# A graph attention kernel: who issues the single rows of the last two batches, and how the last batch's products and copies are laid out

## The chip, the cores and the metric

The kernel runs on one core of a Trainium2 chip. The metric is the device time of one execution in microseconds (us). Each run is one execution. A profile of one execution stands beside it; its times are counted from the start of its span.

## The reference

The reference is one layer of graph attention with a residual. There are 12,500 nodes of 128 values and 412,500 edges, sorted by their target `dst`, each with 64 values of its own. There are four heads of 32 values.

```python
h = jnp.maximum(_layernorm(x, axis=-1), 0.0)
h = (h @ W_node.T).reshape(num_nodes, H, HD)
e = (edge_attr_64 @ W_edge.T).reshape(num_edges, H, HD)
att = jnp.sum(concat([h[src], h[dst], e], -1) * a, axis=-1)
att = jnp.where(att > 0, att, 0.2 * att)
m = jnp.maximum(segment_max(att, dst), 0.0)
ex = jnp.exp(att - m[dst])
denom = segment_sum(ex, dst) + (num_edges - deg)[:, None] * jnp.exp(-m)
out = x + segment_sum((ex / denom[dst])[:, :, None] * h[src], dst)
```

## The kernel before

**The data.** A first phase writes a table of one row of 144 values (576 bytes) per node: for each of the four heads 32 values of `h`, two ones and a source logit (35 values, `AW`), and then four target logits. The main phase goes over the edges. 128 edges make a tile, 7 tiles a chunk (461 chunks), and 7 chunks a batch: 66 batches, 0 to 65. The last batch, 65, has six chunks, and the sixth of these has only three tiles. A batch's source rows lie in a tile `hs` with an edge per partition; three buffers of `hs` are used in turn.

**How a batch's rows come in.** Most come by GpSimd (POOL): one indirect DMA gathers the 128 rows of a tile (L636, in `gather`). In batches from 3 on, the first two tiles of an even batch (256 rows) and the first one of an odd batch (128 rows) are left to `row_by_row` (L658 to L662): the addresses are loaded into registers, up to 32 at a time (L658), and each row is then a DMA of its own (L662), issued by the sync engine (SP) or by ScalarE (ACT). A DMA is issued by the engine in whose program it stands, in the order of that program. The constants: `SPROWS` 112, `FRONT` 64, `ACTROWS` 80. In iteration b of the main loop, SP issues up to 64 rows of batch b+1 ahead of `load_near` (L585), then, behind the loads of `eft` (L576, L577), the rest of batch b+1 and rows of batch b+2, up to 112 in all, and leaves 80 rows of batch b+2 over. ACT issues these 80 at the end of iteration b, behind everything else that ACT does in that iteration. So the 256 rows of batch 64 are issued as 112 by SP and 80 by ACT in iteration 62, and 64 by SP in iteration 63; the 128 of batch 65 as 48 by SP and 80 by ACT in iteration 63. In iteration 64 SP has no rows to issue.

**What is done with a batch b.** Each engine takes its instructions in order.

- `weigh` (L718): VectorE (DVE) waits until the rows have landed (`landed`, L670), adds source and target logits (L746), and goes through a leaky unit (L751, L754), two scans along the edges of a target (L757, L759) and a subtraction (L760). ACT takes the exponential (L762). Beside it DVE makes L766. DVE then transposes the result back (L768, L770, L772). `load_pen` (L677, by SP) fetches the next batch's marks of where a target begins, once L766 has read the old ones.
- `scatter` (L813): DVE multiplies the rows by the weights, chunk by chunk (L822), and TensorE (PE) sums the products by target with a matrix `hot` of 0 and 1 (L829).
- For the next batch ACT spreads the target logits over `pick` (L594, once `load_near` has landed), DVE chooses among them (`choose`, L598 to L611) and makes `hot` (`mark`, L714), and PE makes the edges' share `z` (L695).
- `collect` (ACT, L851) copies each chunk's sums from PSUM into `r`, one copy of 32 partitions for each head and chunk. `merge` (L863 to L900) runs along the chunks and adds to the accumulator `acc`. In iterations 62 to 64 both stand at the end of the batch's own iteration. `finish` (L971 to L993) turns finished targets into output rows; a store (L996, by SP) and the next load of `x` (L956, by SP) follow.

**The last batch** has a path of its own, `end_in_parts` (L774): its first four tiles of each chunk (`EARLY`) are done as part 0 and the other three as part 1, so that part 0 can begin while part 1's rows are on their way. For each part DVE weighs (the lines of `weigh_part`) and multiplies (L796). PE makes for each chunk and tile one product of `hot` (128 by 32) with the whole row of 140 values (L802), into 32 partitions at position `at` of PSUM, four chunks in one tile `pa`. ACT then copies 32 partitions by 35 values for each chunk and head into `r` (L810): 24 copies for part 0, and 20 for part 1, where the sixth chunk has no tiles and DVE clears its place in `r` (L807). These copies stand, in the program, ahead of the next part's `weigh_part`. `merge` (from L863) and `finish` come behind it. In `finish` of this end PE makes 16 products at positions `s * W` that change from one product to the next (L988).

Of the kernel before, what the change touches and what calls it, by code (L numbers as in the profile page):

```python
# [9 lines left out]
F32 = mybir.dt.float32  # L10
# [6 lines left out]
ENG = mybir.EngineType  # L17

P = 128
# [4 lines left out]
H = 4  # L24
# [7 lines left out]
CB = 2 * SB - 1  # L32
NBT = -(-NCH // CB)
# [6 lines left out]
W = 32  # L40
G = 4
# [12 lines left out]
AW = HD + 3  # L54
HB = HD + 1
EROW = H * AW
ROW = EROW + H
SPLIT = 2 * AW
RUN = (G - 1) * ROW + SPLIT
# [11 lines left out]
ACTROWS = 80  # L71
# [4 lines left out]
def tiles_of(c):  # L76

    return 0 if c >= NCH else T if c < NCH - 1 else LAST
# [12 lines left out]
def by_row(b):  # L91

    return (2 if b % EVERY == 0 and b < NBT - 1 else 1) if LOOSE < b < NBT else 0


def merges():
# [36 lines left out]
def kernel(  # L133
# [12 lines left out]
    nc = tc.nc  # L146
# [87 lines left out]
    with (  # L234
# [210 lines left out]
        pa = pp1.tile([P, 2 * H], F32, name="pw")  # L445
# [105 lines left out]
    ps = stack.enter_context(tc.tile_pool(name="ps", bufs=1, space=bass.MemoryType.PSUM))  # L551
# [99 lines left out]
    def row_by_row(s, engine, kind, n):  # L651

        last = s.left
        s.left = max(0, last - n)
        some = last - s.left
        while last > s.left:
            first = max(s.left, last - RL, (last - 1) // P * P)
            _, at = nc.values_load_multi_w_load_instructions(  # L658
                row_at[s.b - 2:s.b - 1, first:last], engines=[kind], min_val=0, max_val=(NB * P - 1) * WIDE,
                skip_runtime_bounds_check_because="a src is below N, and N at most NB * P")  # L660
            for i, v in enumerate(at, first):
                by_itself(engine.dma_start(s.hs[i % P:i % P + 1, i // P, :].bitcast(U8),  # L662
                                           table_b[ds(v, WIDE)].rearrange("(o c) -> o c", o=1)),
                          f"lone{s.b}", lone_sems, lone_done, s.b % ROWSEMS)
            last = first
        return n - some
# [107 lines left out]
    def end_in_parts(s):  # L774

        nc.vector.memset(s.pen[:, EARLY * P:EARLY * P + 1], -BIG)
        spans = ((0, EARLY), (EARLY, T))
        r = work.tile([P, AW * (MC + 1)], F32, name="r")
        r = r[:, :AW * (len(spans) * s.chunks + 1)].rearrange("p (d c) -> p d c", d=AW)
        breaks = work.tile([P, s.chunks, len(spans)], F32, name="breaks")  # L780
        nc.vector.memset(breaks, 0.0)
        nc.vector.tensor_copy(breaks[:, :, 0], new[:, s.c0:s.c0 + s.chunks])
        by_chunk = s.hs[:, :, :EROW].rearrange("p (t q) k -> p q t k", q=CB)
        for i, (t0, t1) in enumerate(spans):
            if i:
                landed(nc.vector, "late", late_sems, late_done, 0, s.hs[:, EARLY * CB:, :], s.ends[:, :, :, :])
                weigh_part(s, t0, t1, None)
            else:
                weigh(s, None)
            got = []  # L790
            for q in range(s.chunks):
                held = min(tiles_of(s.c0 + q), t1)
                if held <= t0:
                    continue
                rows = by_chunk[:, q, t0:held, :].rearrange("p t (h k) -> p t h k", h=H)[:, :, :, :HB]
                nc.vector.tensor_tensor(  # L796
                    rows, rows, ex_ps[:, t0:held, q * H:(q + 1) * H, None].to_broadcast([P, held - t0, H, HB]), op=OP.mult)
                if q % G == 0:
                    pa = ps.tile([P, RUN], F32, name="pa", bufs=3)
                at = q % G * W  # L800
                for t in range(t0, held):
                    nc.tensor.matmul(pa[at:at + W, :EROW], s.hot[:, t, q, :], s.hs[:, t * CB + q, :EROW],  # L802
                                     start=(t == t0), stop=(t == held - 1), tile_position=(0, at))
                got.append((q, pa[at:at + W, :]))
            for q in range(s.chunks):
                if tiles_of(s.c0 + q) <= t0:
                    nc.vector.memset(r[:, :, 1 + q * len(spans) + i], 0.0)  # L807
            for q, pa in got:
                for h in range(H):
                    nc.scalar.copy(r[h * W:(h + 1) * W, :, 1 + q * len(spans) + i], pa[:, h * AW:(h + 1) * AW])  # L810
        return r, breaks

    def scatter(s):  # L813
# [240 lines left out]
    def batch(b):  # L1054
        if b not in batches:
            s = batches[b] = Batch()
            s.b = b
            s.c0 = chunk_of(b)
            s.chunks = chunk_of(b + 1) - s.c0
        return batches[b]  # L1060
# [13 lines left out]
    with tc.manual_schedule():  # L1074
        for k in range(AHEAD):
            batch(k).ends = early[k]
        load_near(batch(0))
        batch(0).hs = raw[0]
        load_pen(batch(0))
        load(batch(0))  # L1080
        open_rows(batch(1))
        clear_rows(batch(1))
        gather(batch(1))
        begin(batch(0))
        load(batch(1))
        spread(batch(0))
        choose(batch(0))
        begin(batch(1))
        measure_late(batch(1))
        for b in range(NBT - 1):  # L1090
            s = batch(b)
            batches.pop(b - 2, None)
            before = batches[b - 1] if 1 <= b <= NBT - ALONE else None
            soon = b >= NBT - ALONE
            if AHEAD <= b + 3 < NBT:
                batch(b + 3).ends = index(b + 3)
            front = 0
            if b:
                front = FRONT - row_by_row(batch(b + 1), nc.sync, ENG.SP, FRONT)
            load_near(batch(b + 1))  # L1100
            if before and merge_of(b - 1)[1] == b - 1:
                for b0, n, behind in parts():
                    if behind == b - 1 and not held_x:
                        held_x[b0] = load_part(work, b0, n)
            if b:
                gather(batch(b + 1), scattered.get(b - 2))
            if b + 2 < NBT:
                load(batch(b + 2))
            if b + 2 < NBT:
                open_rows(batch(b + 2))  # L1110
            if b:
                more = max(SPROWS - front, batch(b + 1).left)
                more = row_by_row(batch(b + 1), nc.sync, ENG.SP, more)
                if b + 2 < NBT:
                    row_by_row(batch(b + 2), nc.sync, ENG.SP, min(more, max(0, batch(b + 2).left - ACTROWS)))
            weigh(s, before)
            load_pen(batch(b + 1))
            if b < NBT - 2:
                mark(s)
            for store in stores:  # L1120
                store()
            stores.clear()
            if b == 4 + NG:
                add_windows(counts)
            scatter(s)
            if b == 0:
                rows_late(batch(1))
            spread(batch(b + 1))
            if before:
                close(before, b)  # L1130
            dch = load_chunks(b - 2) if 0 <= b - 2 < NG else None
            choose(batch(b + 1))
            if dch is not None:
                highest(b - 2, dch)
            if b >= NBT - 3:
                mark(batch(b + 1))
            if b + 2 < NBT:
                begin(batch(b + 2))
            if b == 2 + NG:
                counts = count_windows()  # L1140
            if b == 1:
                nc.scalar.copy(acc.rearrange("p q d -> p (q d)"), carry_m.to_broadcast([P, NQ * AW]))
            if soon:
                for b0, n, behind in parts():
                    if behind == b and not held_x:
                        held_x[b0] = load_part(work, b0, n)
                for g in range(2):
                    collect(s, g)
                close(s, b)
            if b + 2 < NBT:  # L1150
                clear_rows(batch(b + 2))
                row_by_row(batch(b + 2), nc.scalar, ENG.Activation, ACTROWS)
        s = batch(NBT - 1)
        for store in stores:
            store()
        stores.clear()
        for b0, n, behind in parts():
            if behind == s.b:
                held_x[b0] = load_part(work, b0, n)
        merged[s.b] = end_in_parts(s)  # L1160
        close(s, NBT - 1)
        for store in stores:
            store()
# [5 lines left out]
    ps = stack.enter_context(tc.tile_pool(name="rest_ps", bufs=1, space=bass.MemoryType.PSUM))  # L1169
# [253 lines left out]
```

## Time and profile before

| | us |
|---|---|
| median of 3 runs | 4031.48 (4031.11 to 4036.24) |
| the profiled execution's own time | 4038.12 |
| its span in the profile | 4036.3 |
| busy in it: POOL / DVE / PE / ACT | 3011.5 / 2379.0 / 1471.9 / 875.2 |

The profile's page gives busy time by engine, 40 slices of the span, the chain of work that ended last, and the costliest groups of instructions. The trace behind it can be asked for a timeline: rows with start, duration, engine, line and operation, output and input tiles, the number of instructions merged into the row, and in brackets the idle time before the row and what ended it. PE is TensorE's matmul, PEld its weight load; an engine's name with a q is its queue of register, wait and DMA-issuing instructions (SPq, ACTq). A row of TensorE counts two records for each product that the program writes.

### The profile page before, as it was taken

How to read it: one execution, taken by the hardware profiler on the slowest of the kernel's cores; microseconds unless marked ns; L12 is line 12 of the kernel's file. 1: busy time of each engine (PE TensorE's matmuls, PEld its weight loads, DVE VectorE, ACT ScalarE, POOL GpSimd, SP SyncE). 2: the span in 40 equal slices, each digit the busy share in tenths (PEclk: the TensorE clock that was granted, in tenths of full speed). 3: DMA queues.
4: the chain of work that ended last, by engine and by line, in shares of the span. 5: the costliest groups of instructions: out<-in, count | busy, mean ns of one | idle time of the engine just before them, and what ended most of it. 6: DMA issues, size and time to landing. Idle time of an engine off the chain costs nothing.

```text
span 4036.3 us, 45376 instructions
## 1 busy us (share of the span) xinstructions
PE 1471.9 (36%) x3512; PEld 577.0 (14%) x3512; DVE 2379.0 (59%) x4319; ACT 875.2 (22%) x2714; POOL 3011.5 (75%) x3205
## 2 busy tenths in 40 slices
PE   5653334443243243333233234234323324324322
PEld 4311111111011011111011111111101101101101
DVE  8676666656555556546546646555655555655565
ACT  5232221222122212212212212212212211211222
POOL 7777777777777777777777777777777777777771
PEclk8776667776676676677576667666667667667666
DMA  8444444434434443334443343443443444343430
GB/s 223 121 102 114 117 109 110 101 93 103 109 90 109 108 110 91 101 88 107 108 110 93 100 103 91 108 109 95 99 107 90 105 108 109 87 105 89 109 92 23
DMA packets 287741, 418.29 MB, mean 104 GB/s; under 512 B 83154, under 2 KB 204430, under 8 KB 287410
## 3 DMA queue, kind: packets, MB, share of 16 engines
q0 software_dynamic: 100128, 230.32, 25.1%
q1 hardware_dynamic: 163696, 174.62, 14.8%
q10 hardware_dynamic: 23586, 10.39, 1.1%
q14 instruction: 301, 2.47, 0.2%
q8 instruction: 30, 0.49, 0.1%
HBM read 399.53 MB, written 15.51 MB: 103 GB/s over the span
## 4 chain that ended last, share of the span: by engine, by line
POOL 50%; issue 19%; DVE 6%; SPq 6%; ACTq 5%; PE 4%; ACT 2%; DMA 1%; DVEq 0%; POOLq 0%
POOL hs L636 50%; ACTq L662 4%; SPq L662 4%; PE pa L829 3%; DVE hs L822 2%; PE z L695 1%; SPq L658 1%; ACTq L658 1%; DMA hs<-table,ends 1%; ACT r L851 1%; ACT both L762 1%; DVE pick L611 1%; DVE hot L714 1%; DVE acc L900 1%; ACT up L986 1%
## 5 line engine op out<-in xcount | busy, mean ns | idle before, releaser
L636 POOL DMA_INDIRECT hs<-table,ends x3062 | 2938.8, 960 | 928.3 <-issue 924.7
L829 PE MATMUL pa<-hs,hot 128*128 128x502 f32 x1820 | 926.2, 673 | 2411.8 <-DVE hs L822 2333.8
L829 PEld LDWEIGHTS pa<-hs,hot 128*128 128x128 f32 x1820 | 396.3, 222 | 2933.8 <-issue 2863.7
L851 ACT COPY r<-pa 32x35 f32<-32x35 f32 x1820 | 380.0, 209 | 1968.7 <-issue 1882.8
L746 DVE TENSOR_TENSOR logits<-hs,pick 128x196 f32<-128x196 f32 (+1 forms) x67 | 32.9, 491 | 1017.2 <-DVEq L670 1016.6
L822 DVE TENSOR_TENSOR hs<-hs,exr 128x924 f32<-128x924 f32 x455 | 472.3, 1107 | 0.0
L695 PE MATMUL z<-eft,wa 128*32 128x512 f32 (+3 forms) x1056 | 443.6, 556 | 28.3 <-DMA eft<-in_ef 28.3
L611 DVE COPY_PREDICATED pick<-exr,lw 128x3136 f32<-128x3136 int32 x66 | 239.8, 3633 | 47.4 <-ACT pick L594 47.3
L611 DVE COPY_PREDICATED pick<-exr,pick 128x1568 f32<-128x1568 int32 (+3 forms) x198 | 230.6, 1165 | 6.8
L762 ACT ACTIVATE both<-a 32x224 f32<-32x224 f32 (+2 forms) x268 | 103.2, 385 | 599.2 <-DVE a L760 529.1
L594 ACT COPY pick<-lw 128x3136 f32<-128x3136 f32 x66 | 184.8, 2800 | 81.8 <-ACTq L670 80.3
L768 DVE STREAM_TRANSPOSE exr<-both 128x224 f32<-128x224 f32 (+1 forms) x67 | 28.3, 423 | 236.0 <-ACT both L762 236.0
L695 PEld LDWEIGHTS z<-eft,wa 128*32 128x32 f32 (+1 forms) x1056 | 95.6, 110 | 378.6 <-issue 353.7
L900 DVE TENSOR_TENSOR acc<-acc,a 128x70 f32 x461 | 108.0, 234 | 69.2 <-issue 50.9
L757 DVE TENSOR_TENSOR_SCAN up<-pen_sb,z 32x896 f32<-32x896 f32 (+1 forms) x67 | 133.3, 1990 | 11.9 <-DMA pen_sb<-pens 9.6
L714 DVE TENSOR_TENSOR hot<-exr,key 128x448 f32<-128x448 f32 (+1 forms) x260 | 129.0, 558 | 9.3 <-PE pa L829 2.3
L759 DVE TENSOR_TENSOR_SCAN m<-pen_sb,up 32x896 f32<-32x896 f32 (+1 forms) x67 | 132.6, 1979 | 2.3
L751 DVE TENSOR_TENSOR a<-z,zst 32x224 f32<-32x224 f32 (+2 forms) x268 | 101.0, 377 | 9.9 <-DVE zst L748 0.5
L766 DVE SCALAR_TENSOR_TENSOR both<-pen_sb,m 32x224 f32<-32x224 f32 (+2 forms) x268 | 100.8, 376 | 2.7
L986 ACT COPY up<-a 32x224 f32<-32x224 f32 (+1 forms) x224 | 74.5, 332 | 35.4 <-DVE a L978 28.7
L246 POOL DMA_INDIRECT hs<-in_x,ends x67 | 63.5, 948 | 20.5 <-issue 20.1
L754 DVE SCALAR_TENSOR_TENSOR z<-a 32x896 f32<-32x896 f32 (+1 forms) x67 | 72.1, 1075 | 2.3
(187 smaller groups left out, 1057.0 us busy)
## 6 DMA issues: line engine op xcount, KB each, us to landing
hs<-table SPq DMA_DIRECT2D x6992, 0.6 KB
eft<-in_ef SPq DMA_DIRECT2D x66, 1344.0 KB
hs<-table ACTq DMA_DIRECT2D x5040, 0.6 KB
hs<-table,ends POOLq DMA_INDIRECT x3062, 2.6
lw<-near SPq DMA_DIRECT2D x461, 64.0 KB
eft<-in_ef SPq DMA_DIRECT2D x66, 224.0 KB
pen_sb<-pens SPq DMA_DIRECT2D x66, 98.1 KB
table<-rows ACTq DMA_DIRECT2D x9, 648.0 KB
```

Of the source, the lines that this page charges most:

```text
L594: nc.scalar.copy(pick[:, :, :s.chunks, :], lw[:, None, :s.chunks, :n].to_broadcast([P, T, s.chunks, n]))
L611: nc.vector.copy_predicated(pick[:, :, :s.chunks, :n], bit[:, :, :, None].to_broadcast([P, T, s.chunks, n]), more)
L636: load = nc.gpsimd.indirect_dma_start(out=s.hs[:n, t * CB + q, :], out_offset=None, in_=table[:, :], in_offset=bass.IndirectOffsetOnAxis(a ...
L662: by_itself(engine.dma_start(s.hs[i % P:i % P + 1, i // P, :].bitcast(U8), table_b[ds(v, WIDE)].rearrange("(o c) -> o c", o=1)), f"lone{s. ...
L695: s.made = own_half(s, nc.tensor.matmul(s.z[:, part], wa3[:n, j, :], s.eft[:n, j, part], start=(j == 0), stop=(j == SB - 1)))
L714: nc.vector.tensor_tensor(s.hot[:, :, q0:q0 + n, :].rearrange("p t q r -> p q t r"), rows_ps[:, None, None, :].to_broadcast([P, n, T, W]), ...
L757: on_half(s, nc.vector.tensor_tensor_scan(up[:, e0:e1], s.pen[:, e0:e1], z, 0.0, op0=OP.add, op1=OP.max))
L762: nc.scalar.activation(both[g * R:(g + 1) * R, 0, t0:t1, :], grouped(att, g), AF.Exp)
L822: nc.vector.tensor_tensor(rows, rows, ex_ps[:, :, q * H:(q + 1) * H, None].to_broadcast([P, T, H, HB]), op=OP.mult)
L829: scattered[s.b] = nc.tensor.matmul(pa, s.hot[:, t, q0:q0 + G, :].rearrange("p q r -> p (q r)"), flat[:, at:at + RUN], start=(t == 0), sto ...
L851: nc.scalar.copy(to, pa[row:row + W, k:k + AW])
L900: nc.vector.tensor_tensor(cols, cols, put[:, i0 + i, :, :], op=OP.add)
```

## The change

There are two edits.

- **Rows.** A new function `act_rows` gives ACT 80 rows in batches up to 63 as before, 40 in batch 64 and none in batch 65. SP takes what is left over, by the rules that stand. Batch 64's rows are then issued as 112 by SP and 40 by ACT in iteration 62, and 64 and 40 by SP in iteration 63; batch 65's as 8 by SP in iteration 63, behind those 40, and in iteration 64 as 64 ahead of `load_near` and 56 behind it, all by SP.
- **The last batch.** For each chunk and tile, four products, one for each head, take the place of one: `hot` with 35 values each, at the head's 32 partitions. All chunks of a part then lie side by side in one tile `pa`, and one ACT copy of 128 partitions by 210 values (`keep`) takes the place of a part's 24 or 20. Part 0's copy stands behind part 1's `weigh_part` in the program. For the chunk without tiles in part 1, DVE clears its place in `pa` instead of in `r`.

```diff
+def act_rows(b):
+    return ACTROWS if b < NBT - 2 else ACTROWS // 2 if b < NBT - 1 else 0
...
     def end_in_parts(s):
...
+        sums = []
+        def keep(i):
+            nc.scalar.copy(r[:, :, 1 + i::len(spans)], sums[i])
         for i, (t0, t1) in enumerate(spans):
             if i:
                 landed(nc.vector, "late", late_sems, late_done, 0, s.hs[:, EARLY * CB:, :], s.ends[:, :, :, :])
                 weigh_part(s, t0, t1, None)
             else:
                 weigh(s, None)
-            got = []
+            if i:
+                keep(i - 1)
+            pa = ps.tile([P, RUN], F32, name="pa", bufs=3)
+            sums.append(pa[:, :s.chunks * AW].rearrange("p (q d) -> p d q", d=AW))
             for q in range(s.chunks):
                 held = min(tiles_of(s.c0 + q), t1)
                 if held <= t0:
+                    nc.vector.memset(sums[i][:, :, q], 0.0)
                     continue
...
-                if q % G == 0:
-                    pa = ps.tile([P, RUN], F32, name="pa", bufs=3)
-                at = q % G * W
                 for t in range(t0, held):
-                    nc.tensor.matmul(pa[at:at + W, :EROW], s.hot[:, t, q, :], s.hs[:, t * CB + q, :EROW],
-                                     start=(t == t0), stop=(t == held - 1), tile_position=(0, at))
-                got.append((q, pa[at:at + W, :]))
-            for q in range(s.chunks):
-                if tiles_of(s.c0 + q) <= t0:
-                    nc.vector.memset(r[:, :, 1 + q * len(spans) + i], 0.0)
-            for q, pa in got:
-                for h in range(H):
-                    nc.scalar.copy(r[h * W:(h + 1) * W, :, 1 + q * len(spans) + i], pa[:, h * AW:(h + 1) * AW])
+                    for h in range(H):
+                        nc.tensor.matmul(pa[h * W:(h + 1) * W, q * AW:(q + 1) * AW], s.hot[:, t, q, :],
+                                         s.hs[:, t * CB + q, h * AW:(h + 1) * AW],
+                                         start=(t == t0), stop=(t == held - 1), tile_position=(0, h * W))
+        keep(len(spans) - 1)
         return r, breaks
...
-                    row_by_row(batch(b + 2), nc.sync, ENG.SP, min(more, max(0, batch(b + 2).left - ACTROWS)))
+                    row_by_row(batch(b + 2), nc.sync, ENG.SP, min(more, max(0, batch(b + 2).left - act_rows(b + 2))))
...
-                row_by_row(batch(b + 2), nc.scalar, ENG.Activation, ACTROWS)
+                row_by_row(batch(b + 2), nc.scalar, ENG.Activation, act_rows(b + 2))
```

## The prediction

> **What bounds the kernel now.** I read the costliest groups first, then POOL's timeline near the end.
>
> ```profile
> L636 POOL DMA_INDIRECT hs<-table,ends x3062 | 2938.8, 960 | 928.3 <-issue 924.7
> 3852.88 0.95 POOL L636 DMA_INDIRECT hs<-table,ends  x1 [0.30 <-issue]
> 3912.87 0.95 POOL L636 DMA_INDIRECT hs<-table,ends  x1 [0.30 <-issue]
> 3914.12 0.95 POOL L636 DMA_INDIRECT hs<-table,ends  x1 [0.19 <-DVE acc L900]
> 3941.13 0.95 POOL L636 DMA_INDIRECT hs<-table,ends  x1 [0.30 <-issue]
> 3959.91 0.94 POOL L636 DMA_INDIRECT hs<-table,ends  x1 [0.30 <-issue]
> ```
>
> POOL issues gathers without a pause: 3062 at 0.96 us, with 0.30 between them. The rows are the last gather of batch 63, the last of 64, and the first, 22nd and 37th of batch 65. The first 22 of these are part 0's, and the last 15 part 1's. POOL ends at 3960.85, and the span at 4036.3. So the last 75 us aren't POOL's, and what the change touches lies there and just before. Next come ACT and DVE in that stretch.
>
> ```profile
> 3847.93 32.92 ACTq L662 DMA_DIRECT2D hs<-table  x80
> 3880.89 1.59 ACT L762 ACTIVATE both<-a 32x224 f32<-32x224 f32 x4 [33.77 <-issue]
> 3917.02 4.25 ACT L986 COPY up<-a 32x96 f32<-32x96 f32 x16 [1.49 <-DVE a L978]
> 3923.41 31.24 ACTq L662 DMA_DIRECT2D hs<-table  x80
> 3954.70 1.59 ACT L762 ACTIVATE both<-a 32x224 f32<-32x224 f32 x4 [33.43 <-issue]
> ...
> 3857.76 0.50 DVE L746 TENSOR_TENSOR logits<-hs,pick 128x196 f32<-128x196 f32 x1 [5.34 <-DVEq L670]
> 3865.64 1.08 DVE L760 TENSOR_TENSOR a<-z,m 32x896 f32<-32x896 f32 x1
> 3882.51 0.43 DVE L768 STREAM_TRANSPOSE exr<-both 128x224 f32<-128x224 f32 x1 [14.29 <-ACT both L762]
> 3922.64 0.37 DVE L746 TENSOR_TENSOR logits<-hs,pick 128x196 f32<-128x196 f32 x1
> 3930.28 1.08 DVE L760 TENSOR_TENSOR a<-z,m 32x896 f32<-32x896 f32 x1
> 3931.29 1.56 DVE L766 SCALAR_TENSOR_TENSOR both<-pen_sb,m 32x224 f32<-32x224 f32 x4
> 3956.32 0.43 DVE L768 STREAM_TRANSPOSE exr<-both 128x224 f32<-128x224 f32 x1 [23.47 <-ACT both L762]
> 3986.79 0.33 DVE L746 TENSOR_TENSOR logits<-hs,pick 128x96 f32<-128x96 f32 x1 [0.21 <-DVEq L670]
> ```
>
> The exponentials (L762) of batches 63 and 64 stand in ACT's queue behind 80 row DMAs each. In batch 64 the argument is ready at 3931.36 (L760's end), but the exponential starts at 3954.70, as the last row has been issued. DVE idles 23.47 us before L768. In batch 63 it idles 14.29 us. Nothing else fills the time, and POOL finishes before DVE needs its rows of batch 65.
>
> **Rows, batch 63's exponential.** 40 row DMAs fewer, at 32.92/80 = 0.41 us with their register loads, take 16.5 us off ACT. Its queue is free at 3864.4, before L760's end at 3866.72. So L762 starts at about 3866.8, 14.1 us earlier, and all that hangs on it in DVE, ACT and PE moves up. How far it carries is set at batch 64's L746, now at 3922.64: without POOL it could start at 3908.5. It needs POOL's last gather of batch 64, which ends at 3913.82. Batch 63 shows how long that takes to be seen: its last gather ended at 3853.83, and L746, which did wait (5.34 us, ended by the wait of L670), started at 3857.76, 3.93 later. So L746 goes to 3917.75: **4.9 us gained**, and the other 9.2 turn into a wait for POOL. The 40 rows that SP takes over are issued from about 3858 (below) and land long before.
>
> **Rows, batch 64's exponential.** ACT's 80 rows in iteration 63 go wholly. L762 starts when L760 has ended, and DVE goes on when L766 has ended (3931.29 + 1.56 = 3932.85). With a pass between engines L768 is at 3933.0 instead of 3956.32: **23.3 us gained**. ACT is done with its work ahead of that (L986 ends at 3921.27), so nothing else holds it.
>
> Together 28.2. Everything behind it moves up by this if nothing new is late. Three things could be. The first is SP, which takes over 80 rows in iteration 64 and also issues there the 40 that it had issued earlier.
>
> ```profile
> 3826.42 23.13 SPq L662 DMA_DIRECT2D hs<-table  x64
> 3850.99 3.42 SPq L585 DMA_DIRECT2D lw<-near  x7
> 3858.06 16.84 SPq L662 DMA_DIRECT2D hs<-table  x48
> 3875.00 0.85 SPq L677 DMA_DIRECT2D pen_sb<-pens  x1
> 3886.34 0.40 SPq L956 DMA_DIRECT2D xg<-in_x  x1
> 3897.84 2.73 SPq L585 DMA_DIRECT2D lw<-near  x6
> 3932.88 0.88 SPq L677 DMA_DIRECT2D pen_sb<-pens  x1
> ...
> SPq L956 <- DMA out<-xg: 11.6, 2, 9.1
> ```
>
> In iteration 63 SP still issues 48 rows (40 of batch 64, 8 of 65), with one register load more: about 1.5 us later behind them. In iteration 64 its 64 rows stand behind the load of `x` at 3886.34, which waits 9.1 us for the store ahead of it (the last row, of the waits: total, times, longest). I add 1.5 for the extra load, 2.8 for the first register load (3823.6 to 3826.42 in iteration 63) and 23.1 for the 64 rows: 3914. The six target loads (L585), now at 3897.84, follow by about 3918.5, and 56 rows at 0.361 with a first load take it to 3941.5. L677 for batch 65 follows at 3942, 9 us later than now. Batch 65's L746 moves to 3986.79 - 28.2 = 3958.6, so the rows and marks have 16 us to land. The target loads are needed by ACT's L594 behind the exponential, at about 3928, and have some 9 us. Each us beyond these margins would be lost one for one.
>
> The second is POOL, whose timeline doesn't change. Part 0's gathers end at 3942.08 and are seen by 3946.0, against 3958.6. Part 1's end at 3960.85 and are seen by 3964.8, against 3970.3 (the row at 3998.53 below, less 28.2). The third is ACT, which gets shorter only. I count no loss, with 5.5 us of margin for part 1 as the tightest.
>
> **The last batch.** Here are its ACT, DVE and PE rows, and how PE stood in that stretch (length, then busy time and records of PE, PEld, DVE, ACT and POOL, then granted clock).
>
> ```profile
> 3998.53 0.27 DVE L746 TENSOR_TENSOR logits<-hs,pick 128x72 f32<-128x72 f32 x1
> 4000.89 5.29 ACT L810 COPY r<-pa 32x35 f32<-32x35 f32 x24 [6.92 <-PE pa L802]
> 4002.78 0.55 DVE L760 TENSOR_TENSOR a<-z,m 32x384 f32<-32x384 f32 x1
> 4006.20 1.16 ACT L762 ACTIVATE both<-a 32x96 f32<-32x96 f32 x4
> 4007.39 0.29 DVE L768 STREAM_TRANSPOSE exr<-both 128x96 f32<-128x96 f32 x1 [3.11 <-ACT both L762]
> 4012.06 4.40 ACT L810 COPY r<-pa 32x35 f32<-32x35 f32 x20 [4.70 <-PE pa L802]
> 4016.49 0.17 DVE L865 TENSOR_SCALAR mc<-r 128x12 f32<-128x12 f32 x1 [5.51 <-ACT r L810]
> ...
> 3995.94 6.03 PE L802 MATMUL pa<-hs,eft 128*32 128x140 f32 x46 [19.21 <-DVE hs L796]
> 4009.11 3.16 PE L802 MATMUL pa<-hs,eft 128*32 128x140 f32 x30 [7.14 <-DVE hs L796]
> 4025.41 1.93 PE L988 MATMUL up<-a,ident 128*32 128x128 f32 x32 [13.14 <-DVE a L978]
> ...
> 3995.90:4002.00 6.10, 6.03 (x46) 4.48 (x46) 5.89 (x14) 1.05 (x6) 0.00 (x0) 0.54 0.01 4
> ```
>
> (1) Part 0's 24 copies hold ACT until 4006.18. Part 1's exponential, whose argument is ready at 4003.33, waits 2.8 us. With the copy behind it, that goes, and PE starts part 1 at 4006.3 instead of 4009.11 (both without the 28.2).
>
> (2) Products. Part 0 gets 184 records of 35 columns for 46 of 140, and part 1 120 for 30. The trace has no such product. From above, 0.105 to 0.131 us a record is what the old ones took, one position at a time. L988 is the nearest row, since its position changes from product to product: 0.060 (1.93/32), or 0.047 without the last record's own length of 0.43 (the row of 429 ns further down). Between them I put it at 0.053. Its 128 columns are 3.7 times the new 35. From below, half of 0.053 would be left if the columns set half of it; that is an estimate. I take 0.040. Part 1's products then take 4.8 and end with 0.3 of run-out at 4011.4. Part 0's take 7.4 from 3995.94, are done by 4003.3, and hide behind DVE's and ACT's part 1.
>
> The Trainium skill, TensorEngine Tiling (Array Packing), Performance Considerations, Instruction Overhead, speaks against such a cut: each matmul has about 60 cycles of overhead, so that one column costs as much as 60, and no tiling factor should be taken from a dimension that is already small. At a half-rate clock of 1.2 GHz (the Trainium skill, TensorE: Matmul & The Clock Gate, Part 1; the row's granted 0.54 agrees) that is an estimate of 0.050 a record: part 1 would take 6.0, and the total come out 1.2 us later. The trace cannot tell this from the load of weights.
>
> (3) Copies. One copy of 128 by 210 values comes behind DVE's clearing of the empty chunk, which waits for the last product.
>
> ```profile
> 3909.47 0.37 ACT L873 ACTIVATE up<-dif 128x231 f32<-128x231 f32 x1 [1.06 <-DVE dif L872]
> ```
>
> 231 values took 0.37, so 210 take 0.35. With 0.1 for the clearing and three passes of 0.1, L865 starts at 4011.4 + 0.75 = 4012.15 instead of 4016.49: **4.3 us gained**, 2.7 at 0.053 and 5.9 at 0.027. From L865 on nothing changes.
>
> **The sum.** 4.9 + 23.3 + 4.3 = 32.5 us. The profiled execution of 4038.12 (span 4036.3) would become 4005.6. It stood 6.6 above the median of the runs. I take the gain off the median: 4031.48 - 32.5 = **3999.0**.
>
> **The rivals.**
>
> - *SP is late.* If its rows in iteration 64 start only when DVE has cleared the next `hs` (L624, which stands just before L746 and so at 3908, instead of 3891), its last row and L677 come at about 3960, and batch 65 starts 2 to 8 us late: some 4004. For it: SP's program is the longest here. Against: no instruction between L956 and the rows reads what DVE writes, and there are 16 us of margin.
> - *PE at the old rate.* With 0.121 us a record (9.19/76), 304 records take 36.8 from 3995.94, and PE becomes the bound: L865 at 4033.5, 17.0 later than now. 28.2 less 17.0 leaves 11.2: 4020.3. Against it: L988's row.
> - *Slower: each change of position empties PE.* A product would then cost a whole record.
>
> ```profile
> L802 PE MATMUL pa<-hs,eft 128*32 128x140 f32 x76 | 9.2, 429 | 26.4 <-DVE hs L796 26.4
> ```
>
> 152 x 0.429 = 65.2: L865 at 4061.9, 45.4 later, which is 17.2 more than the rows give: 4048.7. It decides from (4016.49 + 28.2 - 3995.94 - 0.75)/152 = 0.316 us a product. L988 speaks against it: 16 products with changing positions took 1.93, or 0.12 each. The Trainium skill, TensorEngine Tiling (Array Packing), Key Properties, says that changing the tiling mode drains TensorE, not changing just the tile; by that the price isn't due here, and L988 agrees.
> - *The rows weren't what held ACT.* The profile names no releaser for L762 but "issue". If it waited for something else, only the tail's 4.3 is left: 4027.2. Against: it starts 0.05 us after the last row, both times.
>
> **How the numbers follow.** Forecast 0.74, SP late 0.08, PE at the old rate 0.08, emptied PE 0.05, rows without effect 0.05. A measurement of this kernel tells about 0.2%, or 8.1 us, from no change. The first three are faster by more: 0.90. Rows without effect is within it: 0.05. Emptied PE is slower: 0.05. The range takes the forecast with both record prices (3997.4 to 4000.6), the runs' spread of 5 us on either side, and SP late by up to 8: 3991 to 4012. It leaves out 0.18.
>
> **What would show it.** L762 of batch 64 within 0.2 us of L760's end, and DVE's 23.47 before L768 gone. Batch 64's L746 waiting for L670 some 9 us, at about 3917.8. SP's last row by 3942, and no wait of batch 65's L746. Part 1's exponential ahead of any copy, its products in 3.2 to 6.4 us, and one copy ahead of L865. A DVE wait for L670 in batch 65, or products above 0.12 us a record, would make the forecast wrong.

## The result and the profile after

| | before | after |
|---|---|---|
| median of 4 runs each, us | 4031.30 (4030.05 to 4036.24) | 3993.13 (3990.70 to 3996.44) |
| profiled execution: own time, span | 4038.12, 4036.3 | 3996.44, 3994.7 |

The ratio is 0.9902 (95% interval 0.9886 to 0.9917): faster, by 38.2 us between the medians, and by 33 to 46 us by the interval. The forecast was 3999.0, with a gain of 32.5.

In the kernel after, most lines have moved by 5 or 8: L636 is now L641, L662 L667, L670 L675, L677 L682, L746 L751, L760 L765, L762 L767, L768 L773, L829 L837, L865 L873, L956 L964. Within the rewritten end, L796 is now L811 and L802 L815, and the one copy is L793. These are the rows of its timeline around batch 64: POOL, ACT and DVE.

```profile
3908.88 0.94 POOL L641 DMA_INDIRECT hs<-table,ends  x1 [0.30 <-issue]
...
3845.88 16.03 ACTq L667 DMA_DIRECT2D hs<-table  x40
3863.00 1.59 ACT L767 ACTIVATE both<-a 32x224 f32<-32x224 f32 x4 [17.95 <-DVE a L765]
3921.31 1.59 ACT L767 ACTIVATE both<-a 32x224 f32<-32x224 f32 x4 [18.00 <-DVE a L765]
...
3861.89 1.08 DVE L765 TENSOR_TENSOR a<-z,m 32x896 f32<-32x896 f32 x1
3912.42 0.50 DVE L751 TENSOR_TENSOR logits<-hs,pick 128x196 f32<-128x196 f32 x1 [7.67 <-DVEq L675]
3920.20 1.08 DVE L765 TENSOR_TENSOR a<-z,m 32x896 f32<-32x896 f32 x1
3922.93 0.43 DVE L773 STREAM_TRANSPOSE exr<-both 128x224 f32<-128x224 f32 x1 [0.16 <-ACT both L767]
3952.55 0.32 DVE L751 TENSOR_TENSOR logits<-hs,pick 128x96 f32<-128x96 f32 x1 [0.20 <-DVEq L675]
```

Both exponentials (L767) now name DVE's L765 as what ended the idle time before them, where they named "issue" before. The 23.47 us that DVE idled before batch 64's transpose (L773) are 0.16. In their place DVE idles 7.67 us before batch 64's logits, and the wait for the rows (L675) ends that. POOL's last gather of the batch ended 2.60 us earlier (3909.82 to 3912.42). Batch 65's logits come after 0.20 us of idle time (0.21 before), so nothing new is late for them.

The next rows are SP's, in iteration 64.

```profile
3877.38 0.40 SPq L964 DMA_DIRECT2D xg<-in_x  x1
3880.13 23.36 SPq L667 DMA_DIRECT2D hs<-table  x64
3905.30 2.74 SPq L590 DMA_DIRECT2D lw<-near  x6
3910.38 20.29 SPq L667 DMA_DIRECT2D hs<-table  x56
3930.76 0.85 SPq L682 DMA_DIRECT2D pen_sb<-pens  x1
```

SP's last row is issued by 3930.67 (the end of the 56 rows), 22 us ahead of batch 65's logits. These are ACT's, PE's and DVE's rows of the last batch.

```profile
3969.11 1.16 ACT L767 ACTIVATE both<-a 32x96 f32<-32x96 f32 x4 [9.39 <-DVE a L765]
3970.29 0.36 ACT L793 COPY r<-pa 128x210 f32<-128x210 f32 x1
3974.54 0.36 ACT L793 COPY r<-pa 128x210 f32<-128x210 f32 x1 [3.89 <-DVE pa L808]
...
3961.68 2.69 PE L815 MATMUL pa<-hs,eft 128*32 128x35 f32 x139 [19.20 <-DVE hs L811]
3965.28 0.92 PE L815 MATMUL pa<-hs,eft 128*32 128x35 f32 x45 [0.90 <-issue]
3972.02 2.28 PE L815 MATMUL pa<-hs,eft 128*32 128x35 f32 x120 [5.82 <-DVE hs L811]
...
3964.28 0.27 DVE L751 TENSOR_TENSOR logits<-hs,pick 128x72 f32<-128x72 f32 x1
3970.30 0.29 DVE L773 STREAM_TRANSPOSE exr<-both 128x96 f32<-128x96 f32 x1 [0.27 <-ACT both L767]
3971.19 2.47 DVE L811 TENSOR_TENSOR hs<-hs,exr 128x396 f32<-128x396 f32 x5
3974.93 0.17 DVE L873 TENSOR_SCALAR mc<-r 128x12 f32<-128x12 f32 x1 [0.33 <-ACT r L793]
```

Part 1's exponential runs right behind L765. Part 1's 120 records of products take 2.28 us, no longer than DVE needs to multiply the five chunks (2.47). One copy of 0.36 follows.

Where the time went is seen best by counting from POOL's last gather of batch 64, since where that ends differs from execution to execution (3913.82 before, 3909.82 after, and 3902 to 3913 in the first four experiments).

| stretch | before | after | difference | forecast |
|---|---|---|---|---|
| end of that gather to batch 64's logits | 8.83 | 2.60 | -6.2 | -4.9 |
| to its transposed exponential | 33.68 | 10.51 | -23.2 | -23.3 |
| to batch 65's logits of part 0 | 30.47 | 29.62 | -0.9 | 0 |
| to the logits of part 1 | 11.74 | 11.73 | 0 | 0 |
| to its transposed exponential | 8.86 | 6.02 | -2.8 | -2.8 |
| to the merge's first step | 9.10 | 4.63 | -4.5 | -1.5 |
| to the end of the span | 19.82 | 19.74 | -0.1 | 0 |
| sum | 122.50 | 84.85 | -37.7 | -32.5 |

The rest of the spans' 41.6 us lies ahead of that gather, in POOL's own timeline, whose program is the same in both kernels; 3.3 of these 4.0 us are there already where POOL has done batch 63's gathers (3853.83 and 3850.51).

### The profile page after: what moved, and what is told of

It is laid out like the page before. It is cut to its first block, busy times and chain, and to the rows that moved or that the text cites. A ratio compares the mean times of both kernels' runs of the same rounds, so it can differ in the third digit from the quotient of the medians.

```text
span 3994.7 us, 45788 instructions
## 1 busy us (share of the span) xinstructions
PE 1466.2 (37%) x3740; PEld 577.3 (14%) x3740; DVE 2378.9 (60%) x4319; ACT 866.6 (22%) x2672; POOL 3009.1 (75%) x3205
## 3 DMA queue, kind: packets, MB, share of 16 engines
q1 hardware_dynamic: 163936, 174.69, 14.7%
q14 instruction: 301, 2.47, 0.2%
## 4 chain that ended last, share of the span: by engine, by line
POOL 63%; issue 21%; PE 4%; DVE 3%; SPq 2%; DMA 1%; ACT 0%; POOLq 0%; DVEq 0%; ACTq 0%
POOL hs L641 63%; PE pa L837 2%; PE z L700 1%; SPq L667 1%; DMA hs<-table,ends 1%; DVE hs L830 1%; DVE up L762 0%; DVE m L764 0%; DMA eft<-in_ef 0%; SPq L663 0%; DVE a L756 0%; ACT both L767 0%; DVE hot L719 0%; DVE z L759 0%; DVE a L765 0%
## 5 line engine op out<-in xcount | busy, mean ns | idle before, releaser
L641 POOL DMA_INDIRECT hs<-table,ends x3062 | 2936.4, 959 | 927.1 <-issue 924.8
L837 PE MATMUL pa<-hs,hot 128*128 128x502 f32 x1820 | 921.2, 670 | 2381.1 <-DVE hs L830 2339.2
L837 PEld LDWEIGHTS pa<-hs,hot 128*128 128x128 f32 x1820 | 394.8, 221 | 2899.6 <-issue 2868.3
L751 DVE TENSOR_TENSOR logits<-hs,pick 128x196 f32<-128x196 f32 (+1 forms) x67 | 33.0, 493 | 1012.9 <-DVEq L675 1012.3
L767 ACT ACTIVATE both<-a 32x224 f32<-32x224 f32 (+2 forms) x268 | 103.2, 385 | 569.6 <-DVE a L765 566.7
L773 DVE STREAM_TRANSPOSE exr<-both 128x224 f32<-128x224 f32 (+1 forms) x67 | 28.3, 423 | 204.2 <-ACT both L767 204.2
L762 DVE TENSOR_TENSOR_SCAN up<-pen_sb,z 32x896 f32<-32x896 f32 (+1 forms) x67 | 133.3, 1990 | 11.2 <-DMA pen_sb<-pens 8.9
```

The source lines that it names most:

```text
L641: load = nc.gpsimd.indirect_dma_start(out=s.hs[:n, t * CB + q, :], out_offset=None, in_=table[:, :], in_offset=bass.IndirectOffsetOnAxis(a ...
L762: on_half(s, nc.vector.tensor_tensor_scan(up[:, e0:e1], s.pen[:, e0:e1], z, 0.0, op0=OP.add, op1=OP.max))
L767: nc.scalar.activation(both[g * R:(g + 1) * R, 0, t0:t1, :], grouped(att, g), AF.Exp)
L837: scattered[s.b] = nc.tensor.matmul(pa, s.hot[:, t, q0:q0 + G, :].rearrange("p q r -> p (q r)"), flat[:, at:at + RUN], start=(t == 0), sto ...
```

## The experiments

Theory A is this table, with the reason for its first two rows: ACT's row DMAs stood ahead of the exponentials, and once they are gone, POOL's last gather of batch 64 is what the end hangs on. The rivals were that the gain beyond the forecast came from the rows (B), that the wait for POOL takes part of the gain already when batch 65's rows alone leave ACT (C), that the two parts of the rows' edit simply add up (D), and that SP or ACT is still the bound (E). The first four experiments were on one chip, on which the kernel before takes 4040.82 us.

**Each edit alone.** `e1_rows_only` has the rows' edit and the old `end_in_parts`.

> The edit of the rows alone; the last batch's products and copies are those of the kernel before. Theory A, read from the two traces: the rows are worth 6.2 us at batch 64's wait for its rows, 23.2 at its exponential and 0.9 in its sums on TensorE, so about 30 us below the kernel before (4001); the last batch's part makes up the other 7 to 8. Rival B: the last batch is worth the 4.3 us forecast, and what the change gained beyond the forecast also comes from the rows: about 34 us below (3997).

Measured: 4010.44 us against 4040.82, ratio 0.9927 (0.9913 to 0.9940), so 24 to 35 us. By the trace, the first two stretches are 2.66 and 10.51 as in the changed kernel, and the last batch's 8.86 and 9.17 as in the kernel before. Theory A holds in these stretches. The 0.9 that it expected in batch 64's sums is not there (30.87 to batch 65's logits, 30.47 before). The time alone doesn't exclude rival B's 34.

`e2_end_only` has the new `end_in_parts` and ACT's 80 rows in all batches.

> The edit of the last batch alone; ACT keeps 80 rows of each batch. Theory A: 2.8 us from part 1's exponential, which no longer stands behind 24 copies, and 4.5 from the products and the one copy: about 7.3 us below the kernel before (4024). Rival B: 4.3 us below (4027), with products at about 0.040 us a record. In the trace, A expects four records in about 0.058 us.

Measured: ratio 0.9983 (0.9974 to 0.9992), so 3 to 11 us. That allows both figures. The trace decides: part 1's stretches are 6.03 and 4.62, 7.3 less than before, and its products are these.

```profile
4003.89 2.28 PE L810 MATMUL pa<-hs,eft 128*32 128x35 f32 x120 [5.68 <-DVE hs L806]
```

That is 0.019 us a record, not 0.040. Rival B falls: the extra gain in the tail comes with the products and the one copy.

**The two parts of the rows' edit.** In `e3_row65_only` only batch 65's rows leave ACT.

```diff
-    return ACTROWS if b < NBT - 2 else ACTROWS // 2 if b < NBT - 1 else 0
+    return ACTROWS if b < NBT - 1 else 0
```

> Of the rows' edit only batch 65's part: ACT issues 80 rows of batch 64 as before and none of batch 65; the last batch as before. Theory A: batch 64's exponential no longer stands behind the rows, 23 to 24 us below the kernel before (4007 to 4008), and batch 64's logits do not wait for rows. Rival C: the wait for batch 64's rows from POOL takes part of it already here, and less than 20 us is gained.

Measured: ratio 0.9945 (0.9931 to 0.9958), so 17 to 28 us. Batch 64's logits start 13.29 us after POOL's last gather and wait for nothing; the transposed exponential comes 10.38 behind them, 23.3 less than before. The time alone doesn't exclude rival C's less than 20; the trace does, as nothing is waited for.

In `e4_row64_only` only 40 of batch 64's rows leave ACT.

```diff
-    return ACTROWS if b < NBT - 2 else ACTROWS // 2 if b < NBT - 1 else 0
+    return ACTROWS if b != NBT - 2 else ACTROWS // 2
```

> Of the rows' edit only batch 64's part: ACT issues 40 rows of batch 64 instead of 80, and 80 of batch 65 as before; the last batch as before. Theory A: all of ACT's program moves up by 14.1 us, its 80 row DMAs of batch 65 with it. These do not wait for POOL, so batch 64's exponential behind them comes 14 us earlier though its logits can come only about 6 earlier: 14 us below the kernel before (4017). The two parts are then not a sum: 14 and 23 alone, 30 together. Rival D: the parts add up, and this one alone is worth the 6 us that the wait for POOL leaves (4025).

Measured: ratio 0.9961 (0.9948 to 0.9975), so 10 to 21 us. Rival D's 6 is excluded. The rows of its timeline are ACT's and DVE's.

```profile
3908.22 30.89 ACTq L667 DMA_DIRECT2D hs<-table  x80
3939.15 1.59 ACT L767 ACTIVATE both<-a 32x224 f32<-32x224 f32 x4 [33.07 <-issue]
...
3915.18 0.50 DVE L751 TENSOR_TENSOR logits<-hs,pick 128x196 f32<-128x196 f32 x1 [7.67 <-DVEq L675]
```

ACT's 80 rows of batch 65 start before batch 64's logits, which wait for POOL. The exponential is still late, but by less: the two stretches are 2.26 and 25.59, against 8.83 and 33.68. 14.7 us are gained here, where 6.6 of them lie at the logits and 8.1 at the exponential. Alone, the parts are worth about 14.7 and 23.3; together 29.4. They overlap by some 8.6 us. ACT's row DMAs start 14.3 us earlier here, counted from that gather, but the logits only by 6.6, as they wait for POOL. The 8.1 that is left shows at the exponential, and that time goes anyway when batch 65's rows leave ACT.

**The layout of the last batch.** The runs from here on were on two other chips, on which the kernel before takes 6975 and 6967 us, 1.73 times as long (more of this at the end), so their times say nothing of steps of a few us, and their traces are read for stretches that depend on the tail alone. On such a chip the changed kernel itself (`e11_changed_again`) has 6.03 us to part 1's transposed exponential and 4.63 to the merge, as on the first (6.02 and 4.63).

`e5_order_only` is the changed kernel with the old products and copies, but part 0's copies behind part 1's weighing.

```diff
         def keep(i):
-            nc.scalar.copy(r[:, :, 1 + i::len(spans)], sums[i])
+            for q, pa in kept[i]:
+                for h in range(H):
+                    nc.scalar.copy(r[h * W:(h + 1) * W, :, 1 + q * len(spans) + i], pa[:, h * AW:(h + 1) * AW])
...
-                    for h in range(H):
-                        nc.tensor.matmul(pa[h * W:(h + 1) * W, q * AW:(q + 1) * AW], s.hot[:, t, q, :],
-                                         s.hs[:, t * CB + q, h * AW:(h + 1) * AW],
...
+                    nc.tensor.matmul(pa[at:at + W, :EROW], s.hot[:, t, q, :], s.hs[:, t * CB + q, :EROW],
```

> The changed kernel with the last batch's old products (128 by 140 at a chunk's position) and its 24 and 20 copies, but part 0's copies behind part 1's weighing as in the change. Theory A: of the last batch's 7.3 us the order's 2.8 stay and the 4.5 of products and copy are lost: 4 to 5 us above the changed kernel, and 9 us from part 1's transposed exponential to the merge's first step, as in the kernel before, instead of 4.6. Rival: ACT, which now has 44 copies in one piece behind the exponential, is the bound, and the order's 2.8 go too: 7 us above.

Measured: 6952.92 us. The stretch to part 1's exponential is 6.02, as changed, and that to the merge 9.73, against 4.63. ACT's row tells why it is 0.6 more than the old 9.10.

```profile
6930.58 9.71 ACT L794 COPY r<-pa 32x35 f32<-32x35 f32 x44
```

All 44 copies run without a gap behind the exponential, so part 0's now delay part 1's. The order alone is worth 2.8 less 0.6; the products and the one copy are worth 5.1. Theory A's split holds, with a small share of the rival.

`e6_fixed_position` has all tiles of a chunk at one head's position before the next.

```diff
-                for t in range(t0, held):
-                    for h in range(H):
+                for h in range(H):
+                    for t in range(t0, held):
```

> The changed kernel with the loop over heads outside the loop over tiles: the same products, but all tiles of a chunk at one position before the next head's. Theory A: the rate comes from four records under way at four positions (four in 0.058 us). At one position two are under way, as with the old products: 0.029 us a record. A chunk's 24 records then take 0.70 us, more than DVE's 0.49 for a chunk, part 1's products take about 3.5 us instead of 2.3, and the end comes 1.2 us later. Rival: only the 35 columns count, and the records come as fast as with changing positions.

It ran once, so only its trace is used.

```profile
6924.94 3.15 PE L815 MATMUL pa<-hs,eft 128*32 128x35 f32 x120 [4.96 <-DVE hs L811]
```

3.15 us for 120 records instead of 2.28, 0.026 a record, and 5.46 to the merge instead of 4.63; part 0's 184 took 5.37, 0.029 a record. The order of the products is thus what makes the records cheap enough to hide behind DVE; theory A was right in kind and a little high in size (3.5). That the changing position does it is the likely reason, but this order also follows each `hot` by another one, where in the change four products in a row have the same; the run doesn't part the two.

**What the end hangs on now.** `e7_pool_4_less` and `e8_pool_12_less` leave out gathers of batch 64, 4 and 12 of them, as do `e9_pool_4_less` and `e10_pool_12_less`. This is the edit for 4.

```diff
+                out = s.b == NBT - 2 and t * CB + q >= T * CB - 4
-                if t >= tiles_of(s.c0 + q) or rows_of(s.c0 + q, t) < P:
+                if out or t >= tiles_of(s.c0 + q) or rows_of(s.c0 + q, t) < P:
                     nc.vector.memset(s.hs[:, t * CB + q, :], 0.0)
-                if t < tiles_of(s.c0 + q) and t * CB + q >= (RAW[s.b] if s.b < 2 else by_row(s.b)):
+                if not out and t < tiles_of(s.c0 + q) and t * CB + q >= (RAW[s.b] if s.b < 2 else by_row(s.b)):
                     s.tiles.append((t, q))
```

> The changed kernel without four of POOL's 47 gathers of batch 64; these tiles are zeros, so their edges are left out of the sums. Theory A: behind the change the end hangs on POOL's last gather of batch 64, and DVE has 7.7 us of idle time there. Four gathers are 5.0 us: 5 us below the changed kernel (3988). Rival E: the end hangs on SP's or ACT's work, and the time stays at 3993.

> The changed kernel without twelve of POOL's 47 gathers of batch 64; these tiles are zeros, so their edges are left out of the sums. Twelve gathers are 15 us. Theory A: the gain ends where DVE's idle time of 7.7 us is used up, about 8 us below the changed kernel (3985), and DVE no longer waits for rows of batch 64. Rival: the whole 15 us (3978), if what DVE does ahead of that wait has slack of its own.

Measured: 6935.72 and 6935.14 us. In these executions POOL's last gather of batch 64 ended 138 and 141 us ahead of its logits, so POOL was no bound there, and the runs tell nothing of the question. The same two kernels were run again, together with the changed kernel, on the other chip of that kind.

> The kernel of the run with four gathers of batch 64 less (their tiles are zeros, their edges left out) once more, beside the changed kernel itself on the same chip: in the run before, the single row DMAs of SP and ACT were served far slower on that chip and set its time, so it told nothing of POOL. Theory A: the end hangs on POOL's last gather of batch 64, with 7.7 us of idle time in DVE there: 5 us below the changed kernel. Rival E: the end hangs on SP's or ACT's work: no difference.

> Twelve gathers of batch 64 less (their tiles are zeros, their edges left out), likewise once more. Theory A: about 8 us below the changed kernel, as DVE's idle time ahead of batch 64's logits is then used up. Rival: the whole 15 us.

> The changed kernel itself, as the reference of this call: some 38 us below the kernel before, as in its first runs, if the chip serves the row DMAs as there.

Measured: 6936.40, 6923.53 and 6940.18 us, with 24 to 35 us between the fastest and the slowest run of each; again the gathers end 139 us or more ahead. On this chip the changed kernel stands at 0.9949 (0.9934 to 0.9965) of the kernel before, so 24 to 46 us are gained, and the expected 38 lies within. That taking gathers away shortens the end stays untried on a chip of the first kind. What speaks for it is the wait itself: in the changed kernel, `e1_rows_only` and `e4_row64_only`, whose ACT rows differ, the logits follow POOL's last gather by 2.60, 2.66 and 2.26 us, and in the kernels whose DVE comes later by 8.8 to 13.3. The chain of work that ended last also goes through this gather in the changed kernel; these are its pieces there (start, duration, what).

```profile
3908.88 2.90 DMA hs<-table,ends
3911.99 0.44 issue
3912.42 0.51 DVE logits L751
```

It reaches the gather's data by way of POOL's gathers, one behind the other, and no row DMA of SP or ACT stands in it between them and the logits.

**One step further.** `e12_by_head_64` makes batch 64's sums like the last batch's.

```diff
+        if s.b == NBT - 2:
+            pa = ps.tile([P, RUN], F32, name="pa", bufs=3)
+            s.sums.append(pa[:, :s.chunks * AW].rearrange("p (q d) -> p d q", d=AW))
...
+                for t in range(T):
+                    for h in range(H):
+                        scattered[s.b] = nc.tensor.matmul(pa[h * W:(h + 1) * W, q * AW:(q + 1) * AW], s.hot[:, t, q, :],
+                                                          s.hs[:, t * CB + q, h * AW:(h + 1) * AW],
+                                                          start=(t == 0), stop=(t == T - 1), tile_position=(0, h * W))
+            return
...
+            if g == 0:
+                nc.scalar.copy(merged[first][0][:, :, 1:], s.sums[0])
```

> The changed kernel with batch 64's sums made in the same way as the last batch's: products head by head at changing positions, and one copy of 128 by 245 values in place of 28 of 32 by 35. Theory A: 392 records at 0.015 us are 5.7 us, less than DVE's 7.3 for the seven chunks, so the sums are ready before DVE has chosen and marked for batch 65; the merge's first step no longer waits 4.5 us for ACT's copies. About 4 to 4.5 us below the changed kernel; part 1's rows from POOL are then just in time. Rival: PE cannot keep that rate over 392 records, or the products wait for instructions, and nothing is gained.

Measured: 6948.34 us, not to be told from 6940.18. On this chip there was nothing to gain: the wait of 4.5 us for ACT's copies, which the step was to take out, isn't there in the changed kernel either. DVE waits for `pick` ahead of it (`e11_changed_again`), and then comes to the merge's first step without idle time.

```profile
6899.31 3.13 DVE L616 COPY_PREDICATED pick<-exr,lw 128x2688 f32<-128x2688 int32 x1 [26.65 <-ACT pick L599]
...
6908.19 0.17 DVE L873 TENSOR_SCALAR mc<-r 128x7 f32<-128x7 f32 x1
```

The PE rows of `e12_by_head_64` tell of the rate alone.

```profile
6852.24 0.81 PE L836 MATMUL pa<-hs,hot 128*32 128x35 f32 x40 [24.98 <-issue]
...
6855.32 0.22 PE L836 MATMUL pa<-hs,hot 128*32 128x35 f32 x1 [1.90 <-issue]
6857.43 0.21 PE L836 MATMUL pa<-hs,hot 128*32 128x35 f32 x1 [1.89 <-issue]
...
6868.65 3.90 PE L836 MATMUL pa<-hs,hot 128*32 128x35 f32 x249 [0.50 <-issue]
```

Where instructions come without gaps, 249 records take 3.90 us, 0.0157 each, so PE keeps the rate. But seven records stand alone here, 0.7 to 2.8 us apart, with nothing to wait for but "issue". Whether the step gains on the first kind of chip is open.

## Why the prediction was right, point by point

- *Batch 63's exponential, 4.9 forecast, 6.2 measured.* The mechanism was as put: the exponential started at 3863.00, as L765 had ended, and the wait for POOL took the rest (7.67 us of idle time, 9.2 forecast). The term that was mis-sized is how long after POOL's last gather its rows are seen: 3.93 was taken from batch 63, 2.60 was measured, and 2.26 to 2.66 in the two experiments that have this wait.
- *Batch 64's exponential, 23.3 forecast, 23.2 measured.* Right in each row, and confirmed alone by `e3_row65_only`.
- *Nothing new is late.* Right. SP was done 11 us before the forecast. The load of `x` was issued 3.37 us after the store ahead of it, not 10.37 as before, and the store itself came at 3874.01, where 3875.97 and 1.5 more was reckoned. Why the store landed sooner isn't known. The rival of a late SP had no part.
- *Part 1's exponential, 2.8 forecast and measured.*
- *Products, the step that was mis-sized.* It put a record at 0.040 us and PE as what ends part 1 (4.8 us). Measured: 0.019, about DVE's pace (0.021, its 2.47 us over 120 records); 0.0157 where DVE doesn't hold PE up (`e12_by_head_64`). So products and copy gave 4.5 us instead of 1.5. The choice between the two ends was the error: L988's 0.053 scaled with the columns, 0.053 x 35/128 = 0.0145, would have come close. From 128 columns to 35 the price fell in nearly the same ratio (3.4, the columns 3.7), so hardly any part of it stayed, where the prediction let at least half stay.
- The Trainium skill, TensorEngine Tiling (Array Packing), Performance Considerations, Instruction Overhead, gives each matmul about 60 cycles, at the prediction's 1.2 GHz an estimate of 0.050 us. The prediction set this beside a record, but a product has two. By the product, 0.050 is near what the order of `e6_fixed_position` costs (0.052), and the stream with changing positions goes below it: 0.031 (`e12_by_head_64`), both at a granted clock of 0.50. The Trainium skill, same page, Key Properties, has it that a change of tile doesn't drain TensorE, and these two figures agree: changing positions are the cheaper way.
- *The sum.* 37.7 by the stretches against 32.5: 1.3 from the landing, 3.0 from the products, and 0.9 from batch 64's sums on PE. These took 13.87 us here at a granted clock of 0.87, and 14.61 to 14.98 at 0.80 to 0.82 in the kernel before and the first four experiments, so neither edit alone brings it, and for the forecast it is luck. The forecast's gain of 32.5 is thus somewhat low: the measured interval starts at 33. The lower end of the range, 3991, is also not what its own terms give (3997.4 less 5 is 3992.4); 3993.13 lies above both.

## What to carry to other kernels

An engine's queue of DMA issues is work like any other: 80 small DMAs at 0.39 us (31.24/80) held an exponential for 23 us, though ACT was 22% busy. Move them to a queue that has time to spare (SP's was done 22 us ahead here), and look up which wait comes next: two such edits can overlap, as these did by 8.6 us, where one ends at a wait that another engine sets. And a copy for each of many small pieces can be bought off with a layout in PSUM that one copy takes out, if TensorE can make it at a pace that hides.

## What the runs showed of the hardware that wasn't expected

Products of 128 by 32 with 35 columns, in fp32, cost 0.0157 us a record when the position changes from product to product (`e12_by_head_64`), and 0.026 to 0.029 when a chunk's products of one position come first (`e6_fixed_position`).

On two of the chips the same programs took 1.73 times as long. Single operations are no slower there (POOL's gathers 0.95 us, as elsewhere), but engines stand still between instructions for no wait that the profile shows. The chain that ended last is another one there, too: SP's and ACT's queues have 35% and 15% of the span in it, mostly with their row DMAs, where POOL has 63% in the changed kernel on the first chip. SP's 48 rows of iteration 61 took 68.71 us there, and 17.08 on the first chip. These are ACT's rows in the changed kernel there.

```profile
6775.89 0.22 ACT L859 COPY r<-pa 32x35 f32<-32x35 f32 x1 [0.75 <-issue]
6776.59 0.22 ACT L859 COPY r<-pa 32x35 f32<-32x35 f32 x1 [0.48 <-issue]
6777.29 0.21 ACT L859 COPY r<-pa 32x35 f32<-32x35 f32 x1 [0.49 <-issue]
6778.00 0.21 ACT L859 COPY r<-pa 32x35 f32<-32x35 f32 x1 [0.50 <-issue]
6779.41 0.21 ACT L859 COPY r<-pa 32x35 f32<-32x35 f32 x1 [1.20 <-issue]
```

They start 0.70 us apart, or twice that, where the same copies follow each other at 0.22 elsewhere; PE's single records above are mostly three or four times 0.70 apart. A fixed price for each instruction in some stretches fits this, but what it is for wasn't tested and stays open.
